# Halving projection and feed-forward pieces over two steps of a hand-ordered masked-attention kernel

## The chip, the cores and the metric

One core of a Trainium2 chip runs the whole program: 8 samples of a graph-attention layer with a feed-forward block. The metric is the device time of one execution in microseconds; lower is better.

## The reference, cut to what matters

For each of F = 8 samples (f), N = 2048 rows of C = 256 channels, H = 8 heads of D = 32 channels:

```python
qkv = jnp.einsum('fnc,ck->fnk', x, w_qkv)
...
scores = jnp.einsum('fnhd,fmhd->fhnm', q, k) / jnp.sqrt(jnp.asarray(D, x.dtype))
scores = jnp.where(mask, scores, jnp.asarray(-1000000000.0, x.dtype))
attn = jax.nn.softmax(scores, axis=-1)
t = jnp.einsum('fhnm,fmhd->fnhd', attn, v).reshape(F, N, C)
x = _layernorm(x + t, ln1_g, ln1_b)
h = jax.nn.relu(jnp.einsum('fnc,cd->fnd', x, w1) + b1)
f_out = jnp.einsum('fnd,dc->fnc', h, w2) + b2
x = _layernorm(x + f_out, ln2_g, ln2_b)
```

The mask is one 2048 x 2048 adjacency matrix, the same for all samples. A last layer norm of the input plus this result follows. All of it is float32.

## The kernel before, in words

**Items, steps and groups.** The attention is cut into 1024 items (f, qc, g, mb): sample f, a chunk qc of 512 query rows (4 of them), a set g of four heads (2), and a block mb of 128 key rows (16). The 16 items of one (f, qc, g) are called a group here; there are 64, numbered in order, and those with g = 0 are the even ones. The main loop (L455 to L478) takes one step per item. A step t writes, in this order, the instructions of

1. at most one job for the shared PSUM bank, taken from a list of unfinished work (`advance`, L386; not when mb is 0);
2. `scores` (L215) of item t + 2: four products on TensorE (L223) into two PSUM tiles, the mask added by VectorE in two instructions (L226) into a tile `p` in SBUF, and one exp on ScalarE (L228). It fills three rotating pairs of banks;
3. `values` (L232) of item t: four products (L240) that add up over the group's 16 steps in a bank of its own; at mb = 15 ScalarE copies the sum out (L244);
4. `add_up` (L253): the softmax denominators. The 16 `p` tiles of a group are not summed by TensorE one by one. GpSimd adds six of them onto the first (L260), and two chains of three are added by accumulating DMAs that GpSimd issues (L257), onto tiles 1 and 2. Four tiles remain: 14, 1, 2 and 0.

The `p` tiles come from a pool of 10 buffers. A buffer can be written again when its last reader is done: the values product, the addition on GpSimd or by DMA, or, for the four that remain, the ones-products (below).

**The shared bank.** Two banks change roles at each group: one holds the group's values, and the other is left for everything else. It has one buffer, so a job's first product waits until the result of the job before has been read out of it. The jobs:

- `turn` and `turn_rows` (L164, L155): transposes of an input chunk, L160, read out by ScalarE (L161);
- `queries` and `project`, both by `channels` (L177): 128 channels of 512 rows as two products, L180, read out by ScalarE (L182); and, in `project`, the values' projection as eight products of 128 columns, L205, read out by ScalarE (L208);
- `denominator` (L284): ones-products that add the four remaining tiles over the key rows, sixteen products L294 in two halves of eight, one per step, read out by ScalarE (L296) after the second; then a transpose L301 of that result, read by VectorE (L306 to L308);
- `outcome` (L313): two transposes L324, read by VectorE (L325), and a DMA issued by GpSimd that adds the input (L328);
- `tail` (L332): the layer norms and the feed-forward block: transposes L341 (ScalarE, L342), two hidden halves L352 (ScalarE, L353), two output halves L362 (VectorE, L364); between and after them `norm` (L263: VectorE L267 and L268, GpSimd L271 to L275, ScalarE L278), products and sums on GpSimd (L344, L346, L367, L369), an accumulating DMA (L371) and the store (L374, on SyncE's queue);
- in the first sample also the blocks of the mask (L136).

**What sets the order.** There is no scheduler: each engine executes in the order in which the program is written. The jobs are Python generators; `yield BANK` asks for the shared bank, `yield n` sleeps n steps, and other marks wait for input buffers or for a place among the tails. `fill` is sorted by due step. `advance` lets every generator run on as far as it can, and grants the bank to the first that asks, once per step. Denominators are due at once and go first, three steps into the next group when nothing is late. Where a projection is not written when its keys' scores come up, `advance` is called again within the step (L471). What is left after the last item is worked off at the end (L480).

Of the kernel before, what the change touches and what calls it, by code (L numbers as in the profile page):

```python
# [10 lines left out]
F32 = mybir.dt.float32  # L11
# [7 lines left out]
P = 128  # L19
H = 8  # L20
D = 32
CH = 512
# [3 lines left out]

SUM_MIN = 1e-25
SUM_MAX = 1e19
BANK, TURNED, ROOM, INPUTS = -1, -2, -3, -10

MASKED = -57344.0

# [21 lines left out]
def fast_path(ctx, tc, cst, x, adj, out, RS):  # L54
    nc = tc.nc
    F, N, C = x.shape
    NCK, TPC, MB = N // CH, CH // P, N // P
# [5 lines left out]
    kp = ctx.enter_context(tc.tile_pool(name="kp", bufs=2 * NCK + 2))  # L63
    qp = ctx.enter_context(tc.tile_pool(name="qp", bufs=2 * NCK + 2))
# [10 lines left out]
    ctx.enter_context(tc.manual_schedule())  # L75

    ident, identb, wqkv, w1s, w2s = cst["ident"], cst["identb"], cst["wqkv"], cst["w1s"], cst["w2s"]
    state = {"pair": 0, "side": None, "turn": 0, "turned": False, "tails": 0}

    def score_pair():  # L80
        i = state["pair"]
# [21 lines left out]
    def give(t):  # L103
        live[:] = [None if u is t else u for u in live]
# [42 lines left out]
    QT, KT, V, XT = {}, {}, {}, {}  # L147
    XD = [dp.tile([NCK, P, 2, CH], F32, name=f"xd{f}") for f in range(F)]

    def queries(f, c, xT):  # L150
        for g in range(2):
            yield BANK
            QT[f, c, g] = channels(qp, "qT", xT, g * P)

    def turn_rows(xc, xT):  # L155
        for a in range(2):
# [17 lines left out]
        yield from queries(f, c, xT)  # L174
        give(xT)

    def channels(pool, name, xT, k0):  # L177
        ps = bank()
        for a in range(2):
            nc.tensor.matmul(ps, wqkv[:, a, k0:k0 + P], xT[:, a, :], start=(a == 0), stop=(a == 1))  # L180
        t = pool.tile([P, CH], F32, name=name)
        nc.scalar.copy(t, ps)  # L182
        return t

    def reload(f, c):
        while (f, c) not in XT:
            yield 1
        yield INPUTS - 1
        xT = take([P, 2, CH], F32)
        nc.sync.dma_start(xT, XD[f][c])  # L190
        yield 3
        return xT

    def project(f, c, g, xT=None):
        if xT is None:
            xT = yield from reload(f, c)
            while len(KT) < (2 * f + g) * NCK + c:
                yield 1
        yield BANK
        KT[f, c, g] = channels(kp, "kT", xT, C + g * P)  # L200
        yield BANK
        ps = bank()
        for j in range(TPC):
            for a in range(2):
                nc.tensor.matmul(ps[:, j * P:(j + 1) * P], xT[:, a, j * P:(j + 1) * P],  # L205
                                 wqkv[:, a, 2 * C + g * P:2 * C + (g + 1) * P], start=(a == 0), stop=(a == 1))
        v = vp.tile([P, TPC, P], F32, name="v")
        nc.scalar.copy(v, ps.rearrange("p (j c) -> p j c", c=P))  # L208
        V[f, c, g] = v
        give(xT)  # L210
# [19 lines left out]
    LAST = MB - 1  # L230
# [53 lines left out]
    def denominator(f, qc, g):  # L284
        grp = (f, qc, g)
        terms = [PT.pop((f, qc, g, ALONE))] + [PT.pop((f, qc, g, chain[0])) for chain in MOVED + (POOLED,)]
        yield BANK
        ps = bank()
        for n, term in enumerate(terms):
            if n == 2:  # L290
                yield BANK
            for h in range(4):
                r = D * h
                nc.tensor.matmul(ps[r:r + D, :], cst["ones"], term[:, h, :], start=(n == 0), stop=(n == 3))  # L294
        dT = op.tile([P, CH], F32, name="dT")
        nc.scalar.copy(dT, ps)  # L296
        yield 1
        yield BANK
        ps = bank()
        for j in range(TPC):  # L300
            nc.tensor.transpose(ps[:, j * P:(j + 1) * P], dT[:, j::TPC], ident)  # L301
        if g == 0:
            RC[f, qc] = op.tile([P, TPC, H], F32, name="rc")
        rc = RC[f, qc]
        den = ps.rearrange("p (j c) -> p j c", c=P)[:, :, ::D]
        nc.vector.reciprocal(rc[:, :, 4 * g:4 * g + 4], den)  # L306
        nc.vector.tensor_tensor(RS[:, 0], RS[:, 0], den, ALU.add)
        nc.vector.tensor_tensor(RS[:, 1], RS[:, 1], den, ALU.min)  # L308
        if g == 1:
            begin = items.index((f, qc, g, LAST)) + SUM + 2  # L310
            start(begin, outcome(f, qc), begin)
# [20 lines left out]
    def tail(f, qc, y, xin):  # L332
        yield from norm(y)
        yield TURNED
        state["turned"] = True
        yT = work.tile([P, 2, CH], F32, name="turned")
        for a in range(2):
            yield BANK
            ps = bank()
            for j in range(TPC):  # L340
                nc.tensor.transpose(ps[:, j * P:(j + 1) * P], y[:, j, a * P:(a + 1) * P], ident)  # L341
            nc.scalar.activation(yT[:, a, :], ps, AF.Identity, bias=cst["be1c"][:, a:a + 1], scale=cst["g1c"][:, a:a + 1])  # L342
        yield 1
        nc.gpsimd.tensor_tensor(y, y, rows(cst["g1r"]), ALU.mult)  # L344
        yield 1
        nc.gpsimd.tensor_tensor(y, y, rows(cst["be1b2r"]), ALU.add)  # L346
        hT = work.tile([P, 2, CH], F32, name="hT")
        for d in range(2):
            yield BANK
            ps = bank()  # L350
            for a in range(2):
                nc.tensor.matmul(ps, w1s[:, a, d * P:(d + 1) * P], yT[:, a, :], start=(a == 0), stop=(a == 1))  # L352
            nc.scalar.activation(hT[:, d, :], ps, AF.Relu, bias=cst["b1s"][:, d:d + 1], scale=1.0)  # L353
        state["turned"] = False
        yield 1
        z = y
        for jj in range(0, TPC, 2):
            yield BANK
            ps = bank()
            for j in range(jj, jj + 2):  # L360
                for d in range(2):
                    nc.tensor.matmul(ps[:, (j - jj) * C:(j - jj + 1) * C], hT[:, d, j * P:(j + 1) * P], w2s[:, d, :],  # L362
                                     start=(d == 0), stop=(d == 1))
            nc.vector.tensor_tensor(z[:, jj:jj + 2, :], ps.rearrange("p (b c) -> p b c", c=C), z[:, jj:jj + 2, :], ALU.add)  # L364
        yield 1
        yield from norm(z)
        nc.gpsimd.tensor_tensor(z, z, rows(cst["g2r"]), ALU.mult)  # L367
        yield 1
        nc.gpsimd.tensor_tensor(z, z, rows(cst["be2r"]), ALU.add)  # L369
        yield 1  # L370
        nc.gpsimd.dma_start(z, xin, accum_op=ALU.add)  # L371
        yield 7
        yield from norm(z)
        nc.sync.dma_start(out[f, qc * CH:(qc + 1) * CH, :].rearrange("(p j) c -> p j c", p=P), z)  # L374
        state["tails"] -= 1


    fill = []
# [4 lines left out]

    def advance(t, banks):  # L386
        inputs = True
        for e in list(fill):
            while e[0] <= t:
                if e[2] == BANK:  # L390
                    if not banks:
                        break
                    banks -= 1
                elif e[2] < INPUTS:
                    inputs = inputs and not any(u is not None for u in live[:INPUTS - e[2]])
                    if not inputs:
                        break
                elif e[2] == TURNED and state["turned"] or e[2] == ROOM and state["tails"] == 2:
                    break
                e[2] = next(e[1], None)  # L400
                if e[2] is None:
                    fill.remove(e)
                    break
                if e[2] > 0:
                    e[0] = t + e[2]

    def mask_ahead(qc):
        for mc in range(NCK):
# [46 lines left out]
    for t, (f, qc, g, mb) in enumerate(items):  # L455
        if mb == 0 and t:
            state["side"] = 1 - state["side"]
        if f == 0 and g == 0 and mb == 0 and qc + 1 < NCK:
            start(t, mask_ahead(qc + 1), t + 28)
        if g == 1 and mb == 0 and (f or qc == NCK - 1) and (f + 1 < F or qc + 1 < NCK):  # L460
            load_mask(f + (qc + 1) // NCK, (qc + 1) % NCK)
        if f + 1 < F:
            for what, *which in NEXT.get((2 * qc + g, mb), []):
                due = t + MB // 2 if what is turn else items.index((f + 1, 0, which[1], which[0] * TPC)) - LEAD - 1
                start(t, what(f + 1, *which), due)
        if mb:
            advance(t, 1)
        if t + LEAD < len(items):
            nf, _, ng, nmb = items[t + LEAD]
            t0 = t  # L470
            while (nf, nmb // TPC, ng) not in V:  # L471
                advance(t0, 1)
                t0 += 1
            scores(items[t + LEAD])
        values(items[t])
        add_up(items[t])
        if mb == LAST:
            start(t + SUM, denominator(f, qc, g), t)  # L478
    t = len(items)
    while fill:  # L480
        t += 1
        advance(t, 1)


@with_exitstack
# [233 lines left out]
```

## Time and profile before

| | us |
|---|---|
| three timed runs | 3729.24, 3730.40, 3743.26 (median 3730.4) |
| the profiled execution | 3733.92 |
| its span, first to last instruction | 3732.1 |
| TensorE busy (PE) | 3241.8 |
| VectorE busy (DVE) | 2760.8 |
| GpSimd busy (POOL) | 2599.1 |
| ScalarE busy (ACT) | 2411.0 |
| granted TensorE clock | 0.977 of full |

Busy is the time in which an engine has an instruction running. PE rows are products, PEld rows weight loads. In the timeline each row has its start and its length in us, the engine, the line, what is written and read, and how many instructions were merged; in brackets stands how long the engine was idle before it and what ended that. A float32 product appears as two PE instructions, so that a job of two products 128x512 is x4, and a step's scores or values are x8.

### The profile page before, as it was taken

The numbers are of one execution on the slowest core, as the hardware profiler recorded it, in microseconds if no ns is written. First come the engines' busy times: TensorE is split into PE (matmuls) and PEld (weight loads), VectorE is DVE, ScalarE is ACT, GpSimd is POOL, SyncE is SP. The second block draws the span as 40 slices with busy tenths as digits, with TensorE's granted clock in tenths as the row PEclk, the third lists the DMA queues.
The fourth block names the chain that finished last, engine by engine and source line by source line (L and its number), as shares of the span: only waits on it lengthen the run. The fifth ranks groups of instructions, "written<-read, shape, count | busy, mean of one in ns | idle before, by whom it ended". The sixth has DMA issues, their size and how long they took to land. (4 is left out here: it accounts for less than half of the span.)

```text
span 3732.1 us, 53786 instructions
## 1 busy us (share of the span) xinstructions
PE 3241.8 (87%) x22020; PEld 1038.8 (28%) x22020; DVE 2760.8 (74%) x3203; ACT 2411.0 (65%) x1921; POOL 2599.1 (70%) x1363
## 2 busy tenths in 40 slices
PE   7877888899988899889998899889898889988884
PEld 4222223222322233222332223222232222322221
DVE  4777766877688766788677777777768877688883
ACT  3554555766667666766666776666666676677663
POOL 2555666777677775877667785777777777687775
PEclk9998999999999999999999999999999999999997
DMA  6766675776766775776766776676676676676664
GB/s 185 175 142 152 146 175 117 168 162 142 173 150 145 158 171 145 169 153 154 169 138 151 163 172 158 140 165 154 147 175 141 148 171 152 154 164 140 139 134 86
DMA packets 113774, 573.31 MB, mean 154 GB/s; under 512 B 10833, under 2 KB 27729, under 8 KB 60273
## 3 DMA queue, kind: packets, MB, share of 16 engines
q0 software_dynamic: 64848, 436.90, 58.1%
q1 hardware_dynamic: 47856, 131.61, 10.0%
q8 instruction: 174, 2.85, 0.3%
q10 hardware_dynamic: 816, 1.31, 0.1%
q14 instruction: 80, 0.65, 0.0%
HBM read 129.37 MB, written 37.75 MB: 45 GB/s over the span
## 5 line engine op out<-in xcount | busy, mean ns | idle before, releaser
L226 DVE TENSOR_TENSOR p<-s,mask 128x1024 f32<-128x1024 f32 x2048 | 2410.3, 1219 | 753.8 <-PE s L223 480.0
L228 ACT ACTIVATE p<-p 128x2048 f32<-128x2048 f32 x1024 | 1957.1, 1911 | 1232.9 <-DVE p L226 916.2
L260 POOL TENSOR_TENSOR p<-p 128x2048 f32<-128x2048 f32 x384 | 1835.9, 4810 | 653.6 <-ACT p L228 645.0
L223 PE MATMUL s<-qT,kT 32*128 32x512 f32 x8192 | 1193.2, 652 | 232.5 <-DVE p L226 231.0
L240 PE MATMUL x<-p,v 128*32 128x512 f32 x8192 | 1112.2, 616 | 0.0
L257 POOL DMA_DIRECT2D p<-p x384 | 382.7, 1018 | 351.2 <-ACT p L228 138.9
L223 PEld LDWEIGHTS s<-qT,kT 32*128 32x128 f32 x8192 | 325.3, 186 | 853.6 <-DVE p L226 695.6
L240 PEld LDWEIGHTS x<-p,v 128*32 128x32 f32 x8192 | 162.3, 108 | 795.2 <-issue 645.1
L180 PE MATMUL x<-in,wqkv 128*128 128x512 f32 x472 | 234.6, 620 | 23.1 <-ACT oT L244 10.2
L278 ACT ACTIVATE y<-y,nb,rs 128x256 f32<-128x256 f32 x384 | 224.9, 589 | 38.0 <-POOL nb L275 38.0
L294 PE MATMUL x<-p,ones 128*32 128x512 f32 x2048 | 246.3, 599 | 1.8 <-DVE y L364 0.9
L267 DVE BATCH_NORM_STATS2 st<-y 128x6 f32<-128x256 f32 x384 | 160.1, 417 | 27.1 <-DMA y<-in_x_dram 27.1
L362 PE MATMUL x<-w2s,hT 128*128 128x256 f32 x512 | 127.6, 392 | 45.7 <-ACT oT L244 42.3
L352 PE MATMUL x<-turned,w1s 128*128 128x512 f32 x256 | 128.8, 626 | 20.8 <-ACT hT L353 19.5
L180 PEld LDWEIGHTS x<-in,wqkv 128*128 128x128 f32 x472 | 80.3, 190 | 186.1 <-issue 69.8
L362 PEld LDWEIGHTS x<-w2s,hT 128*128 128x128 f32 x512 | 92.1, 190 | 112.0 <-ACT oT L244 68.6
L205 PE MATMUL x<-wqkv,in 128*128 128x128 f32 x896 | 114.9, 282 | 6.4 <-ACT kT L182 6.3
L205 PEld LDWEIGHTS x<-wqkv,in 128*128 128x128 f32 x896 | 104.2, 192 | 55.0 <-ACT kT L182 34.0
L364 DVE TENSOR_TENSOR y<-x,y 128x512 f32<-128x512 f32 x64 | 44.3, 692 | 94.9 <-PE x L362 94.7
L294 PEld LDWEIGHTS x<-p,ones 128*32 128x32 f32 x2048 | 64.0, 111 | 165.8 <-issue 129.7
L272 POOL TENSOR_TENSOR rs<-rs,mhalf 128x4 f32<-128x4 f32 x96 | 99.3, 1035 | 8.0
L341 PE MATMUL x<-ident,y 128*128 128x128 f32 x256 | 48.0, 299 | 54.5 <-ACT turned L342 38.8
(87 smaller groups left out, 1427.1 us busy)
## 6 DMA issues: line engine op xcount, KB each, us to landing
p<-p POOLq DMA_DIRECT2D x384, 1024.0 KB, 9.7
y<-in_x_dram POOLq DMA_DIRECT2D x64, 512.0 KB, 6.1
in<-xd SPq DMA_DIRECT2D x59, 512.0 KB, 8.0
mask<-md SPq DMA_DIRECT2D x28, 1024.0 KB, 6.6
out_dram<-y SPq DMA_DIRECT2D x32, 512.0 KB, 3.0
in<-in_x_dram SPq DMA_DIRECT2D x28, 512.0 KB, 6.9
xd<-in SPq DMA_DIRECT2D x28, 512.0 KB, 10.0
in<-in_adj_dram SPq DMA_DIRECT2D x24, 512.0 KB, 7.6
```

The source lines that it names most:

```text
L180: nc.tensor.matmul(ps, wqkv[:, a, k0:k0 + P], xT[:, a, :], start=(a == 0), stop=(a == 1))
L205: nc.tensor.matmul(ps[:, j * P:(j + 1) * P], xT[:, a, j * P:(j + 1) * P], wqkv[:, a, 2 * C + g * P:2 * C + (g + 1) * P], start=(a == 0), s ...
L223: nc.tensor.matmul(ps2[half][:, j, :], KT[f, mb // TPC, g][r:r + D, (mb % TPC) * P:(mb % TPC + 1) * P], QT[f, qc, g][r:r + D, :], start=Tr ...
L226: nc.vector.tensor_tensor(pt[:, 2 * half:2 * half + 2, :], ps, MK[f, qc][:, mb, None, :].to_broadcast([P, 2, CH]), ALU.add)
L228: nc.scalar.activation(pt, pt, AF.Exp, scale=1.0 / math.sqrt(D))
L240: nc.tensor.matmul(O[grp][r:r + D, :], V[f, mb // TPC, g][:, mb % TPC, r:r + D], PT[item][:, h, :], start=(mb == 0), stop=(mb == LAST))
L257: nc.gpsimd.dma_start(PT[f, qc, g, chain[0]], PT.pop(item), accum_op=ALU.add)
L260: nc.gpsimd.tensor_tensor(first, first, PT.pop(item), ALU.add)
L267: nc.vector.bn_stats(st, t[:, j, :])
L278: nc.scalar.activation(t[:, j, :], t[:, j, :], AF.Identity, bias=nb[:, j:j + 1], scale=rs[:, j:j + 1])
L294: nc.tensor.matmul(ps[r:r + D, :], cst["ones"], term[:, h, :], start=(n == 0), stop=(n == 3))
L362: nc.tensor.matmul(ps[:, (j - jj) * C:(j - jj + 1) * C], hT[:, d, j * P:(j + 1) * P], w2s[:, d, :], start=(d == 0), stop=(d == 1))
```

## The change

Three marks replace one: `BANK` asks for the bank as before; `MORE` and `HOLD` are given in the middle of a job whose bank is kept. The generator that keeps it is the `holder`. A job that reaches `MORE` goes on in the next step, before anything else, and in that step the bank is granted to nobody else. If, at the end of a step, another generator stands at `BANK` and is due to run, the holder at `MORE` is run on in the same step, so that its job stays whole. At `HOLD` (the ones-products, in the middle as before) it is not run on for another's sake. At the last step of a group, in the repeated calls for late projections and at the end (`finish`), any holder is run to its end. A generator that itself asks for the bank again after its job is not seen as waiting while it is the holder.

`MORE` stands in the middle of `channels` (after the first of two products), of the values' projection (after four of eight), of each hidden half (after the first of two) and of each output half (after two of four). The transposes are not divided. `channels` now stores its result itself.

```diff
-    def channels(pool, name, xT, k0):
+    def channels(store, pool, name, key, xT, k0):
+        yield BANK
         ps = bank()
         for a in range(2):
+            if a:
+                yield MORE
             nc.tensor.matmul(ps, wqkv[:, a, k0:k0 + P], xT[:, a, :], start=(a == 0), stop=(a == 1))
-        t = pool.tile([P, CH], F32, name=name)
-        nc.scalar.copy(t, ps)
-        return t
+        store[key] = pool.tile([P, CH], F32, name=name)
+        nc.scalar.copy(store[key], ps)
...
         for j in range(TPC):
+            if j == TPC // 2:
+                yield MORE
             for a in range(2):
...
             if n == 2:
-                yield BANK
+                yield HOLD
...
             for a in range(2):
+                if a:
+                    yield MORE
                 nc.tensor.matmul(ps, w1s[:, a, d * P:(d + 1) * P], yT[:, a, :], start=(a == 0), stop=(a == 1))
...
             for j in range(jj, jj + 2):
+                if j > jj:
+                    yield MORE
                 for d in range(2):
...
-    def advance(t, banks):
+    def resume(e, t):
+        e[2] = next(e[1], None)
+        state["holder"] = e if e[2] in (MORE, HOLD) else None if state["holder"] is e else state["holder"]
+        if e[2] is None:
+            fill.remove(e)
+        elif e[2] > 0:
+            e[0] = t + e[2]
+
+    def advance(t, free=True, finish=False):
         inputs = True
+        if state["holder"]:
+            free = False
+            resume(state["holder"], t)
         for e in list(fill):
-            while e[0] <= t:
+            while e[2] is not None and e[0] <= t and e is not state["holder"]:
                 if e[2] == BANK:
-                    if not banks:
+                    if not free:
                         break
-                    banks -= 1
+                    free = False
...
-                e[2] = next(e[1], None)
-                if e[2] is None:
-                    fill.remove(e)
-                    break
-                if e[2] > 0:
-                    e[0] = t + e[2]
+                resume(e, t)
+        late = any(e[2] == BANK and e[0] <= t for e in fill)
+        while state["holder"] and (finish or late and state["holder"][2] == MORE):
+            resume(state["holder"], t)
...
         if mb:
-            advance(t, 1)
+            advance(t, finish=mb == LAST)
...
             while (nf, nmb // TPC, ng) not in V:
-                advance(t0, 1)
+                advance(t0, finish=True)
...
-        advance(t, 1)
+        advance(t, finish=True)
```

More of the change, by code (lines that the diff above doesn't have):

```diff
@@ L28 @@
 SUM_MAX = 1e19
-BANK, TURNED, ROOM, INPUTS = -1, -2, -3, -10
+BANK, MORE, HOLD, TURNED, ROOM, INPUTS = -1, -2, -3, -4, -5, -10
 MASKED = -57344.0
@@ L77, in fast_path @@
     ident, identb, wqkv, w1s, w2s = cst["ident"], cst["identb"], cst["wqkv"], cst["w1s"], cst["w2s"]
-    state = {"pair": 0, "side": None, "turn": 0, "turned": False, "tails": 0}
+    state = {"pair": 0, "side": None, "turn": 0, "turned": False, "holder": None, "tails": 0}
     def score_pair():
@@ L151, in queries @@
         for g in range(2):
-            yield BANK
-            QT[f, c, g] = channels(qp, "qT", xT, g * P)
+            yield from channels(QT, qp, "qT", (f, c, g), xT, g * P)
     def turn_rows(xc, xT):
@@ L198, in project @@
                 yield 1
-        yield BANK
-        KT[f, c, g] = channels(kp, "kT", xT, C + g * P)
+        yield from channels(KT, kp, "kT", (f, c, g), xT, C + g * P)
         yield BANK
@@ L290, in denominator @@
             if n == 2:
-                yield BANK
+                yield HOLD
             for h in range(4):
```

## The prediction

> **What bounds the kernel now.** I read the page's first part and groups, then the timeline step by step, then the waits.
>
> ```profile
> PE 3241.8 (87%) x22020; PEld 1038.8 (28%) x22020; DVE 2760.8 (74%) x3203; ACT 2411.0 (65%) x1921; POOL 2599.1 (70%) x1363
> ...
> L226 DVE TENSOR_TENSOR p<-s,mask 128x1024 f32<-128x1024 f32 x2048 | 2410.3, 1219 | 753.8 <-PE s L223 480.0
> ```
>
> No engine is full: the bound changes from step to step. A step without a job lasts 2.55 us, and VectorE sets it: two mask additions of 1.22 us, TensorE 0.4 us idle.
>
> ```profile
> 1176.06 1.14 PE L223 MATMUL s<-qT,kT 32*128 32x512 f32 x8 [0.41 <-DVE p L226]
> ...
> 1177.34 2.36 DVE L226 TENSOR_TENSOR p<-s,mask 128x1024 f32<-128x1024 f32 x2 [0.20 <-PE s L223]
> ...
> 1178.62 1.14 PE L223 MATMUL s<-qT,kT 32*128 32x512 f32 x8 [0.42 <-DVE p L226]
> ```
>
> A step with a whole 2 us job is TensorE's, 3.98 us from job to job:
>
> ```profile
> 1655.74 1.98 PE L180 MATMUL x<-in,wqkv 128*128 128x512 f32 x4
> ...
> 1659.72 1.98 PE L180 MATMUL x<-in,wqkv 128*128 128x512 f32 x4
> ```
>
> By starts of rows (medians of the timeline), from the job to the scores it is 1.91 us for L180 and L352, 1.92 for L362, 1.98 for L205, 0.68 for L324; scores to values 1.07; values to the next job 1.00.
>
> The third bound is the bank. A job's result leaves it by a ScalarE copy, and that copy is written between two exps:
>
> ```profile
> 1646.84 1.14 PE L223 MATMUL s<-qT,kT 32*128 32x512 f32 x8
> ...
> 1648.90 0.66 PE L160 MATMUL x<-ident,in 128*128 128x128 f32 x4
> ...
> 1650.44 1.91 ACT L228 ACTIVATE p<-p 128x2048 f32<-128x2048 f32 x1 [1.15 <-DVE p L226]
> ...
> 1652.25 0.57 ACT L161 COPY in<-x 128x512 f32<-128x512 f32 x1
> ...
> 1652.87 0.66 PE L160 MATMUL x<-ident,in 128*128 128x128 f32 x4 [1.25 <-ACT in L161]
> ```
>
> The scores of 1646.84 are masked and exponentiated; only then is the job of 1648.90 copied out, and the next job may start at 1652.87, 1.25 us late. So a job starts no earlier than 6.03 us after the scores of two steps before. Over all triples of neighbouring jobs where this decides, the timeline has 6.03 to 6.82 us: 6.16 for L301 after the two L294 halves, 6.25 for L180 after L160, 6.63 for three L180, 6.73 behind an L352, whose own read-out is 0.67 us, 6.8 where a norm's L278 (0.59) stands between. I take 6.4 and keep 6.05 and 6.75.
>
> **What the Trainium skill says.** *TensorE: Matmul & The Clock Gate*, "Architectural detail", has ScalarE and VectorE as strict FIFO queues; the copy above, which starts when the exp ends, agrees. *PSUM — Partial Sum Buffer*, "The four PSUM rules", says that accumulation bits stay until the next first product of a group clears that bank and quadrant, so an open group may be left for a step; the L294 halves do that already, at 1.90 us each. *Perfetto Trace Analysis*, "Tensor Engine Instruction", says that matmul ends are estimated; hence I use starts.
>
> **The change, part by part.** The order of the changed program, counted step by step: 108 jobs are halved (70 L180, 20 L205, 15 L352, 3 L362); steps without a job fall from 333 to 230. Ones-products stay two halves in two steps: nothing.
>
> 1. *TensorE's side.* A half job from start to scores: L324 needs 0.68 for a quarter of the columns of a 1.91 job, so some 0.2 us is fixed and a half is 0.2 + 1.71/2 = 1.06. Two half steps: 2 x (1.06 + 1.07 + 1.00) = 6.26, against a whole and an empty step, 3.98 + 2.55 = 6.53. 108 x -0.27 = **-29 us**. VectorE, 2.4 of the 3.13 us, isn't in the way.
> 2. *The bank behind a second half.* In the order, 85 of the 108 are followed in the very next step by another job, after a read-out by ScalarE: a generator that wants the bank again doesn't count as waiting, so its halved jobs stand in a row. The next job's start is at least 1.06 + 6.4 = 7.46 us after the first half's; TensorE alone would take 6.26. Halving doesn't bring the copy forward: it sits behind the exp of the item whose scores ran with the first half. 85 x 1.20 = **+102** (72 to 132). Scores, values and VectorE's next masks queue behind that product.
> 3. *Such waits behind whole jobs.* Starts later than TensorE's pace add up to 13.9 us behind L180, 24.9 behind L352, 1.6 behind L205 now. Whole jobs of these kinds followed at once by a job fall from 81, 31, 19 to 11, 3, 12: 12 + 22 + 1 = **-35**.
> 4. *The second step of a group.* A job there waits for the copy L244 of the old values, on average 1.53 us past TensorE's pace (59.6 us in 39). 46 groups have one, not 39: **+11**.
> 5. *Late projections.* In the second sample, three steps get an L205 on top of other jobs because a half took its turn. Each waits within its step for the bank, up to 2 us beyond what it saves: **+4** (0 to 6).
> 6. *p buffers.* Jobs come later, so the ones-products start one to four steps later in 26 groups, and four old `p` tiles are held longer. The build's buffers show it: before, one group rewrites a buffer three items after its old tile, six times; after, 26 groups, 47 times (30 GpSimd additions, 17 DMAs). In that one group DMA reuse cost 1.43 and 5.04 us:
>
> ```profile
> 464.43 0.88 POOL L257 DMA_DIRECT2D p<-p  x1
> ```
>
> ```profile
> 475.57 2.36 DVE L226 TENSOR_TENSOR p<-s,mask 128x1024 f32<-128x1024 f32 x2 [5.04 <-DMA p<-p]
> ```
>
>    In the other even groups, item 3's addition ends 1.1 to 2.7 us before item 6 would write, so those hide. Item 4's DMA lands 1 to 4 us after item 7 starts, but the steps between grow about as much (two L362 ahead of the ones-products). I take 0.4 for each of 14 more by DMA: **+6** (0 to 45).
> 7. *Lag of GpSimd and its DMAs.* After the quickest even groups VectorE waits for such a buffer:
>
> ```profile
> 1183.67 2.36 DVE L226 TENSOR_TENSOR p<-s,mask 128x1024 f32<-128x1024 f32 x2 [0.88 <-DMA p<-p]
> ```
>
>    The first steps of odd groups run 37 us over 2.55 in samples 2 to 8, 33 net of shorter next steps. The even groups get longer (one of 48.9 us gains six 2 us jobs), so GpSimd catches up; L328, L367, L369 and L371 come up to three steps later, past the DMAs of tiles 7 and 10 and onto later additions. I count three quarters as regained: **-25** (-33 to 0).
> 8. *Queues and the end.* SyncE's queue holds as many instructions; stores L374, loads L190 and saves L171 shift by a few steps. Nothing there is late: inputs are asked for three steps ahead. If that cover went, a load's 8 us less three steps would show, under 1 us: zero. One more L362 is left after the last item: **+2**.
>
> Sum: -29 + 102 - 35 + 11 + 4 + 6 - 25 + 2 = **+36 us**. The profiled execution took 3733.9 (span 3732.1), so it would be 3770; on the median 3730.4 I predict **3766**, 1.0% slower.
>
> **Rivals.**
>
> - *Heavier: the `p` buffers decide.* If each of the 41 added close reuses costs what the one group showed, 6.5/6 = 1.1 us, item 6 is 45 instead of 6: **3805**. For it: accumulating DMAs there took 7 to 13 us, three quick steps are 7.6. Against: 27 of the 41 are additions of 4.8 us that end in time.
> - *Unchanged.* The bank's price at its low end, 6.05 (72), and all lag regained (-33): +36 - 30 - 8 = -2, **3728**. For it: plain copies without a norm beside them are nearer 6.05 to 6.25.
> - *Faster: the next job isn't held behind a second half.* The place is TensorE between a second half and the job after it, the price 85 x 1.20. A second half ends about 0.9 us earlier in its step than a whole job; were its copy to run ahead of the exp, item 2 would be nothing, the groups would not stretch (the 25 of item 7 stay lost): +36 - 102 + 25 = -41, **3689**. It decides when the wait is under 0.76 us a half for no change, under 0.55 for 0.5% faster, the other items kept. Against: exp and copy are in one queue, in the written order, and L301 behind the L294 halves, a split job already, waits just so.
> - *It doesn't do what it says:* excluded, the order shows the 108 halves.
>
> **How the numbers follow.** About 0.5% (19 us) is what a measurement can tell from no change. Forecast 0.58, heavier 0.12, both slower by more than that; unchanged 0.20; faster 0.10. So faster 0.1, same 0.2, slower 0.7. The range leaves out most of the faster case and the upper half of the heavier one: from 3724 (the unchanged case, 4 us under) to 3808. With price and lag at their bad ends together it would be 3820 and more; I leave that out. The forecast's own range is 3750 to 3795.
>
> **What would show it.** After: 230 empty steps of 2.55 us; half steps of about 3.1 us; after a second half, TensorE idle by about 1.2 us until ScalarE's copy, and the wait of L180 and L205 for ScalarE's qT and kT, 37 and 34 us of weight-load idle now, grown by some 80 in sum; less waiting of VectorE for DMAs at the first steps of odd groups, some at their items 7 to 10 in even ones; the 48.9 us groups at about 59. A half step well over 3.1 us, no idle TensorE after second halves, or jobs in other places would prove me wrong.

## The result and the profile after

The changed kernel takes 3796.8 us (median of four, 3793.8 to 3800.7), the kernel before, timed beside it, 3734.3 (3729.2 to 3743.3): a ratio of 1.0165, with a 95% interval of 1.0141 to 1.0189. That is 62.5 us slower. The profiled executions, from which all that follows is worked out, took 3796.24 and 3733.92 us, 62.3 apart.

The busy times of the page and the group of mask additions, for the changed kernel (lines are numbered by its own code: L182 was L180, L184 was L182, L207 was L205, L225 was L223, L228 was L226, L259 was L257, L262 was L260, L280 was L278, L326, L327 and L330 were L324, L325 and L328, L356 was L352, L373 and L375 were L367 and L369):

```profile
PE 3248.6 (86%) x22020; PEld 1034.2 (27%) x22020; DVE 2771.7 (73%) x3203; ACT 2411.1 (64%) x1921; POOL 2599.0 (68%) x1363
...
L228 DVE TENSOR_TENSOR p<-s,mask 128x1024 f32<-128x1024 f32 x2048 | 2409.5, 1218 | 835.6 <-PE s L225 482.7
```

No engine has more to do than before. VectorE's additions are as many and as long, but its idle time ahead of them grew from 753.8 to 835.6 us: the loss is waiting. The timeline shows the largest part of it (here both halves of an L182 and the job after them; brackets hold the idle time and what ended it):

```profile
1998.23 1.12 PE L182 MATMUL x<-in,wqkv 128*128 128x512 f32 x2
...
1999.29 1.14 PE L225 MATMUL s<-qT,kT 32*128 32x512 f32 x8
...
2001.35 1.13 PE L182 MATMUL x<-in,wqkv 128*128 128x512 f32 x2
...
2002.99 1.91 ACT L230 ACTIVATE p<-p 128x2048 f32<-128x2048 f32 x1 [0.69 <-ACT y L280]
...
2004.81 0.57 ACT L184 COPY kT<-x 128x512 f32<-128x512 f32 x1
2005.42 1.75 PEld L207 LDWEIGHTS x<-wqkv,in 128*128 128x128 f32 x15 [1.79 <-ACT kT L184]
```

The half step is as short as hoped: 3.12 us from 1998.23 to 2001.35. By the modelled ends the second half has left TensorE by 2002.5, but its copy L184 starts only at 2004.81, when the exp of 2002.99 has ended. The next job starts 4.07 us after the second half, 0.95 later than TensorE's pace.

Three sums over the whole trace are used below. *Bank waits*: start of a job, less the start of the values product of the step before, less 1.00 us (the sums are net: a job that starts a little sooner counts below zero). *Second-step waits*: the same at the second step of a group. *Buffer waits*: start of an item's first mask addition, less the later of VectorE's previous end and the scores' start plus 1.28 us (the distance from 1176.06 to 1177.34 in the prediction's first timeline); what is left is waiting for a `p` tile.

| kernel | time, us | ratio (95%) | bank waits | second step | buffer waits |
|---|---|---|---|---|---|
| before | 3734.3 | 1 | 157.5 | 59.6 | 43.8 |
| changed | 3796.8 | 1.0165 (1.0141 to 1.0189) | 202.8 | 68.3 | 64.2 |
| e2 exp late | 3544.2 | 0.9466 (0.9446 to 0.9486) | 2.4 | 2.1 | 80.9 |
| e4 before, exp late | 3558.6 | 0.9511 (0.9491 to 0.9531) | 7.7 | under 2 | 49.0 |
| e5 ones first, early store | 3815.8 | 1.0195 (1.0176 to 1.0215) | 214.8 | 70.3 | 42.3 |
| e7 before, ones late | 4062.4 | 1.0847 (1.0826 to 1.0868) | 258.6 | 60.4 | 303.8 |
| e12 addition 8 later | 3797.3 | 1.0149 (1.0132 to 1.0166) | 202.7 | 69.1 | 63.2 |

Beside the experiments the kernel before took 3738.5 to 3741.6 us, so times of different rows are compared by their ratios, or by profiled executions. The latter hold some noise of their own: the time ahead of the first values product, where all these programs have the same order but for the place of an exp, is 57.7 us in the profile of the kernel before, 60.2 in the changed one and 61.2 to 65.3 in the experiments. It is called the opening below, and differences of a few us between profiles show nothing. Of the changed kernel's bank waits 80.8 us lie behind second halves, where nothing lay before; those behind undivided L182, L356 and L207 fell from 40.4 to 10.9.

### The profile page after: what moved, and what is told of

The parts are those of the page before. It is cut to its first block, busy times and chain, and to the rows that moved or that the text cites. A ratio compares the mean times of both kernels' runs of the same rounds, so it can differ in the third digit from the quotient of the medians.

```text
span 3794.5 us, 53757 instructions
## 1 busy us (share of the span) xinstructions
PE 3248.6 (86%) x22020; PEld 1034.2 (27%) x22020; DVE 2771.7 (73%) x3203; ACT 2411.1 (64%) x1921; POOL 2599.0 (68%) x1363
## 5 line engine op out<-in xcount | busy, mean ns | idle before, releaser
L228 DVE TENSOR_TENSOR p<-s,mask 128x1024 f32<-128x1024 f32 x2048 | 2409.5, 1218 | 835.6 <-PE s L225 482.7
L262 POOL TENSOR_TENSOR p<-p 128x2048 f32<-128x2048 f32 x384 | 1804.0, 4698 | 643.9 <-ACT p L230 642.9
L225 PE MATMUL s<-qT,kT 32*128 32x512 f32 x8192 | 1191.3, 651 | 219.2 <-DVE p L228 217.0
L259 POOL DMA_DIRECT2D p<-p x384 | 358.9, 974 | 407.4 <-DMA p<-p 197.3
L225 PEld LDWEIGHTS s<-qT,kT 32*128 32x128 f32 x8192 | 325.2, 186 | 814.6 <-DVE p L228 672.4
L182 PE MATMUL x<-in,wqkv 128*128 128x512 f32 x472 | 253.6, 636 | 37.6 <-ACT qT L184 16.0
L280 ACT ACTIVATE y<-y,nb,rs 128x256 f32<-128x256 f32 x384 | 224.8, 589 | 41.8 <-POOL nb L277 41.8
L356 PE MATMUL x<-turned,w1s 128*128 128x512 f32 x256 | 132.4, 631 | 54.4 <-ACT oT L246 27.7
L207 PE MATMUL x<-wqkv,in 128*128 128x128 f32 x896 | 121.7, 286 | 35.4 <-ACT kT L184 19.1
L182 PEld LDWEIGHTS x<-in,wqkv 128*128 128x128 f32 x472 | 74.3, 188 | 224.6 <-issue 90.1
L207 PEld LDWEIGHTS x<-wqkv,in 128*128 128x128 f32 x896 | 107.2, 194 | 100.3 <-ACT kT L184 39.1
L296 PEld LDWEIGHTS x<-p,ones 128*32 128x32 f32 x2048 | 64.4, 110 | 173.9 <-issue 137.2
L343 PE MATMUL x<-ident,y 128*128 128x128 f32 x256 | 44.6, 293 | 63.7 <-ACT turned L344 43.9
L373 POOL TENSOR_TENSOR y<-y,g2r 128x1024 f32<-128x1024 f32 x32 | 83.6, 2611 | 12.8 <-ACT y L280 12.5
## 6 DMA issues: line engine op xcount, KB each, us to landing
xd<-in SPq DMA_DIRECT2D x28, 512.0 KB, 10.2
```

The lines of the kernel that those rows point to most:

```text
L225: nc.tensor.matmul(ps2[half][:, j, :], KT[f, mb // TPC, g][r:r + D, (mb % TPC) * P:(mb % TPC + 1) * P], QT[f, qc, g][r:r + D, :], start=Tr ...
L228: nc.vector.tensor_tensor(pt[:, 2 * half:2 * half + 2, :], ps, MK[f, qc][:, mb, None, :].to_broadcast([P, 2, CH]), ALU.add)
L259: nc.gpsimd.dma_start(PT[f, qc, g, chain[0]], PT.pop(item), accum_op=ALU.add)
L262: nc.gpsimd.tensor_tensor(first, first, PT.pop(item), ALU.add)
L280: nc.scalar.activation(t[:, j, :], t[:, j, :], AF.Identity, bias=nb[:, j:j + 1], scale=rs[:, j:j + 1])
```

## The experiments

### The bank behind the exp

**e2, the exp written later.** Nothing but the place of the exp in ScalarE's queue is changed; jobs, halves and buffers stay.

```diff
-        nc.scalar.activation(pt, pt, AF.Exp, scale=1.0 / math.sqrt(D))
+        state["exp"] = pt
+
+    def exp():
+        pt, state["exp"] = state["exp"], None
+        if pt is not None:
+            nc.scalar.activation(pt, pt, AF.Exp, scale=1.0 / math.sqrt(D))
...
             advance(t, finish=mb == LAST)
+        exp()
```

> The changed kernel with one edit: the exp of an item is written one step later, after the job of the next step and its read-out, ahead of the next scores; all else is in the same order. So a job's ScalarE copy no longer stands behind the exp of the item whose scores ran in the step before. Theory A, the bank is held behind the exp: the 81 us of waits behind second halves, and most of the 11 behind whole jobs and of the 45 and 48 behind the two kinds of transposes that ScalarE reads out, go; the time falls by 75 to 140 us, to 3655 to 3720. Theory B, the wait is not the exp's but the copy's own length and what VectorE does, or the later exp delays the values product as much: the time stays within 15 us of the changed kernel, or rises.

Measured: 3544.2 us, 5.3% below the kernel before; its profiled execution of 3543.3 is 253 us below that of the changed kernel. Theory A holds, and its estimate was far too low. At the same place of the program as above, the trace of this kernel (L235 is the exp):

```profile
1863.85 1.12 PE L182 MATMUL x<-in,wqkv 128*128 128x512 f32 x2
...
1865.01 0.59 ACT L184 COPY kT<-x 128x512 f32<-128x512 f32 x1 [0.71 <-PE x L182]
1865.95 1.91 ACT L235 ACTIVATE p<-p 128x2048 f32<-128x2048 f32 x1 [0.36 <-DVE p L228]
...
1866.97 1.86 PEld L207 LDWEIGHTS x<-wqkv,in 128*128 128x128 f32 x16 [0.84 <-issue]
```

Now ScalarE waits for the product and copies it at once; the exp follows at 1865.95, and the next job starts 3.12 us after the second half, not 4.07. Bank waits are gone (202.8 to 2.4; those behind second halves from 80.8 to nothing), and so are those of the second step (68.3 to 2.1), which I had not counted: the copy of the old values stood behind an exp as well. Together that is 266.6 us, of which buffer waits take 16.7 back.

**e4, the same edit on the kernel before** (nothing divided).

> The kernel before with the exp written one step later, after the next step's job and read-out; nothing is divided. If the bank behind the exp is what the division pays for, undivided jobs gain less from this edit than divided ones: they have 40 us of waits behind whole jobs and 98 us behind the two kinds of transposes, so the time falls by 50 to 120 us, to 3615 to 3685. Against the changed kernel with the same edit this shows what the division is worth once the bank wait is gone: by item 1 of the forecast 29 us, less 9 for the second step of a group and what the p buffers cost, so between 0 and 20 us in favour of the division. If the edit does nothing here, the transposes' waits are not the exp's.

Measured: 3558.6 us; between the profiled executions (3733.9 and 3554.5) 179 us. So much did the exp ahead of the copies cost without any halves. With the exp late, the division gains 11 us between the profiles and 0.45% by the ratios (0.9466 against 0.9511, the intervals just apart), within the 0 to 20 us expected: the sign of the change turns once the exp no longer stands ahead of the copies. Halving costs 62 us with the exp there and gains 11 without, so some 73 us of its cost hang on that one place.

**e10, only queries and keys divided** (the other three `yield MORE` removed), and **e9, only the values' projection divided** (the other three removed).

> The changed kernel with only the queries' and keys' projections divided: 71 halved jobs, 70 of them followed at once by another job. By the measured prices: 71 x -0.27 = -19 us; 70 x +0.92 = +64; whole jobs followed at once fall from 117 to 40 (L182 of the changed kernel) and from 61 to 38 (L356), some -17; second steps of a group with a job 47 instead of 39, +10; 3 more close reuses by DMA at 1.3, +4: +42 us, a ratio of 1.011. If bank waits were the smaller part of the loss and the pushed-back feed-forward and p buffers the larger, it is under +25, a ratio under 1.007, since close reuses are 24 instead of 47.

> The changed kernel with only the values' projection divided: 19 halved jobs, of which 6 are followed at once by another job, 12 close reuses of p buffers. Theory A, what costs is the bank behind a second half that a job follows: 19 x -0.27 = -5 us, 6 x +0.92 = +6, three more close reuses by addition and none by DMA: nothing; the time is that of the kernel before within 8 us, a ratio of 0.998 to 1.002. Theory B, each division costs by itself, wherever it stands (62.5 us over 108 halves, 0.58 each): +11 us, a ratio of 1.003.

e10: 1.0099 (1.0080 to 1.0119), 38 us between the medians and 42.5 between the profiled executions, near the sum of 42 by the measured prices and above the 25 of its rival. Bank waits behind second halves are 64.4 us in 70, the 0.92 each that were put in; that part of the sum is confirmed. The rest of the match is in part luck: 5.3 of the 42.5 us are the opening, and buffer waits fell by some 15 us where 4 more were expected. e9: 1.0051 (1.0032 to 1.0070), 20.3 us between the profiles, 5.1 of them the opening. That misses theory A's nothing and also B's 11. Its waits view names another wait, TensorE for a reloaded input (its L180 is the changed kernel's L182):

```profile
PE x L180 <- DMA in<-xd: 17.3, 6, 3.8
```

Six times the halves shift a load so that the product asks for it up to 3.8 us too early, 17.3 us in all (0.2 in the kernel before). Behind the six second halves that a job follows stand 5.6 us, as A has it. But the main loop, from the first values product to the last, grew by only 11 us, since buffer waits fell by some 12, and no run took the input's wait alone away; so e9 doesn't decide between A and B.

**e11, exp late with only the projections divided** (feed-forward whole).

> The changed kernel with the exp written after the next step's job, and the feed-forward pieces left whole: 91 halved projections, 243 empty steps, 25 close reuses of p (47 with all divided). With the exp late no bank wait is left, so each half that is not made costs the 0.27 us of item 1: 17 fewer, +5 us; the fewer close reuses and late projections give back some 10 to 20. So 3530 to 3542, if the p buffers count; 3544 to 3552 if not.

Measured: 3540.2 us, 0.9460 (0.9434 to 0.9486). That is at the upper end of the range for buffers that count, but from e2 it can't be told apart, so the time says nothing on the buffers. Both are the fastest versions found, 5.3 to 5.4% under the kernel before.

### The p buffers and the lag

**e1, ones-products first.** In 26 groups of the changed kernel they start late because a tail's due step ties with theirs and stands ahead in the list.

```diff
-            start(t + SUM, denominator(f, qc, g), t)
+            start(t + SUM, denominator(f, qc, g), t - 1)
```

> The changed kernel with one edit: the ones-products are due one step earlier in the list of work, so that they go ahead of the feed-forward jobs with which they tie. Counted in its order: 107 divided jobs and 230 empty steps as in the changed kernel, 89 of the 107 followed at once by a job (88 there), but ones-products begin at step 3 of the group in 60 of 62 groups (37 there), and close reuses of p buffers fall from 47 to 5. Theory A, the p buffers: the 30 us that bank waits and steps do not explain come from ones-products that start late and keep four old p tiles; then VectorE's waits for DMAs on p (56.7 us) and GpSimd's (197 us) go back to about 26 and 112, and the time falls by 20 to 35 us, to 3762 to 3777. Theory B, the forecast's own item 6: close reuses are nearly all hidden and cost 6 us, the rest is lag of GpSimd that was never regained; then the time is 3785 to 3797.

Measured: 3894.9 us, 1.0408 (1.0388 to 1.0427): 93 us slower than the changed kernel between the profiles, against both theories. The waits of VectorE show a place that was not in either:

```profile
DVE y L327 <- DMA out_dram<-y: 77.9, 21, 6.6
```

The feed-forward jobs now come later, so the tail's store leaves later, and the next outcome wants a `y` tile whose store has not landed; L327 stands in VectorE's queue, and bank waits behind the transposes L326 grow from nothing to 86 us. (The clock granted to TensorE was 0.968 in this run, against 0.977.)

**e3, both edits.**

> Both edits on the changed kernel: ones-products due one step earlier, and the exp written after the next step's job. If bank waits and p buffers are two separate costs, the two gains add up: the time is that of the changed kernel less the gain of each alone (within 10 us). If the p buffers' waits come only because bank waits push the ones-products, the second edit adds under 8 us to the gain of the first. By theory A of both, 3630 to 3695.

Measured: 3574.9 us, 0.9552 (0.9534 to 0.9571), 32 us slower than e2 alone between the profiles. The gains don't add, because the second is a loss.

**e5 and e8, the store three steps earlier**, to take that wait away: `yield 7` ahead of the last norm becomes `yield 4`, on e1 and on e3.

> The changed kernel with ones-products due one step earlier, as in the first experiment, and the pause ahead of a tail's last norm cut from 7 steps to 4, so that the tail's store is issued three steps earlier. In the first experiment VectorE waited 77.9 us (21 times) at the output of the next outcome for the store of an old y tile, and GpSimd and TensorE behind it. Theory A: that wait was the whole of the loss there, and below it the ones-products in time do save what late ones cost; close reuses of p stay at 5 instead of 47, so the 22 us of VectorE's waits at items 6 to 9 go to under 8, the wait for the store goes to under 5, and the time is 3770 to 3790. Theory B: feed-forward jobs pushed back cost as much by themselves (their additions on GpSimd fall on the start of odd groups); then it stays within 8 us of the changed kernel or is slower, 3790 to 3815.

> The changed kernel with the exp written after the next step's job, ones-products due one step earlier, and the pause ahead of the last norm cut from 7 steps to 4. The exp alone gave 3544. With the store in time the 26 us of waits behind outcome's transposes and VectorE's 19 us for the store of y are gone. If the p buffers are a cost of their own, 12 to 30 us are gained on the exp alone, 3514 to 3532; if not, the time stays within 8 us of 3544.

e5: 3815.8 us, 19 slower than the changed kernel between the profiles, 5 of them the opening, and with ratios whose intervals overlap; e8: 3560.7, 0.9510 (0.9485 to 0.9534), 15 slower than e2, 3 of them the opening. The wait for the store is down to 8.5 us in e5 and buffer waits fall by 22 us as expected (at items 6 to 9 from 24.4 to 7.9), and still the time doesn't fall. Against that gain stand 12 us more of bank waits and 7 at the end after the last item, where more is left. Some 15 us stay open; GpSimd now stands 95.8 us at L330 for the outcome's product (30.2 in the changed kernel) and 83.8 at L373 (12.5), but what of that reaches the path I could not separate. So late ones-products cost some 22 us at the buffers, and putting them first costs at least as much elsewhere.

**e7, late ones-products without halves.** On the kernel before, `start(t + SUM + 2, ...)`.

> The kernel before with one edit: ones-products may start two steps later (steps 5 and 6 of the group instead of 3 and 4), nothing is divided. Counted in the build: close reuses of p buffers 130 instead of 6, whole jobs followed by jobs hardly fewer (237 instead of 243). It prices the p buffers without divided jobs. By the trace of the changed kernel (some 21 us of added waits at items 6 to 9 for 41 added close reuses, 0.5 each) it is 62 us slower, about 3800; by the forecast's item 6 (6 us for 41) 18 us, 3755; by the heavier rival (1.1 each) 136 us, 3870.

Measured: 4062.4 us, 8.5% slower, above every estimate. Its waits of VectorE:

```profile
DVE p L226 <- DMA p<-p: 306.2, 82, 8.6
```

In the kernel before this line reads 25.8 us in 19 (19 waits, the middle number). Buffer waits rise by 260 us for 124 added close reuses, 2.1 each, most of it (some 220 us) at item 7, and bank waits by 101. (The clock granted to TensorE was 0.951 in this run, 0.977 in the two kernels compared.) A close reuse in an otherwise quick group costs twice what the heavier rival took. The changed kernel probably escaped because its late ones-products sit in groups that jobs have lengthened; no run tests that.

**e6, without scale and shift of the second norm.** L373 and L375 are left out, so the second norm's gain and shift aren't applied.

> The changed kernel without the scale and shift of the second layer norm (the multiplication L373 and the addition L375 on GpSimd, some 2.6 us each, are left out; the steps between are kept, so every other instruction has its place). In the changed kernel these two lie at steps 0 to 2 of the fourth and sixth group of a sample; before they lay at steps 14 and 15 of the third and fifth. VectorE's waits for p buffers there are 10.5 and 15.2 us over samples 2 to 8. Theory A, the lag wasn't regained but moved with these two: those 26 us fall to under 8 and the time by 20 to 35 us, to 3762 to 3777. Theory B, the lag comes from the chains of additions alone: the waits there stay over 15 us, and the time falls by under 12.

Measured: 3793.2 us, 1.0132 (1.0112 to 1.0151), not to be told from the changed kernel; waits at the start of the fourth and sixth groups 11.8 and 16.1 us, not less. My theory of the lag fell: these two additions aren't its cause.

**e12, GpSimd's addition of item 8 behind item 9's DMA.** In the changed kernel, the third group of the fifth sample ends so (GpSimd's part of the timeline, then VectorE's; L259 issues an accumulating DMA):

```profile
2107.09 2.11 POOL L259 DMA_DIRECT2D p<-p  x2
2109.16 4.62 POOL L262 TENSOR_TENSOR p<-p 128x2048 f32<-128x2048 f32 x1
2117.42 0.88 POOL L259 DMA_DIRECT2D p<-p  x1 [3.64 <-ACT y L280]
```

```profile
2122.65 2.36 DVE L228 TENSOR_TENSOR p<-s,mask 128x1024 f32<-128x1024 f32 x2 [2.27 <-DMA p<-p]
```

The x2 are the DMAs of items 9 and 10, 0.5 us apart; the single one is item 12's. The mask addition at 2122.65 is item 1 of the next group; in the build it takes the buffer of item 10, so it waits for that DMA to land.

```diff
-        if mb in POOLED[1:]:
-            first = PT[f, qc, g, POOLED[0]]
-            nc.gpsimd.tensor_tensor(first, first, PT.pop(item), ALU.add)
+        for pb in ([] if mb == 8 else [8, 9] if mb == 9 else [mb]):
+            if pb in POOLED[1:]:
+                first = PT[f, qc, g, POOLED[0]]
+                nc.gpsimd.tensor_tensor(first, first, PT.pop((f, qc, g, pb)), ALU.add)
```

> The changed kernel with one swap in GpSimd's queue: the addition of item 8 is written behind the DMA of item 9 instead of ahead of it; every other instruction keeps its place, and so do all buffers. In the changed kernel the third and fifth group of a sample became only 4.6 and 1.4 us longer (47.2 to 51.8, 50.3 to 51.7), while their DMA of item 9 is issued at 37.9 and 37.8 us of the group (32.3 and 33.9 before), behind the first norm, the input's DMA and the 4.8 us addition of item 8; the chain's last DMA, item 12's, waits for it and starts at 48.5, 3.3 us before the group ends. Theory A, VectorE's waits for p at the start of the next groups (10.5 and 15.2 us from sample 2 on) come from that place in the queue: item 9's DMA starts 3 to 4 us earlier, item 12's 2 to 4, the waits in these two groups fall from 25.7 to under 13, the time by 10 to 20 us: 3777 to 3787, a ratio of 1.011 to 1.014. Theory B, the transfers' own length decides, or the addition, now later, holds item 11's buffer instead: the waits stay over 20 or move on to items 10 and 11, and the time stays within 8 us of the changed kernel.

Measured: 3797.3 us, not to be told from the changed kernel. Item 9's DMA starts 1.2 us earlier in the third and 2.5 in the fifth group; the waits behind the third fall from 10.5 to 4.5 us, those behind the fifth stay (15.2, 15.4). So the queue's place is part of the cause in the third group. In the fifth it isn't: there, in samples 3 to 7, item 9's DMA lands 48.9 to 49.3 us into the group in both kernels, though it is issued 2 to 3 us earlier in this one. Something on the side of the DMAs decides there, theory B in the main; which transfers, no run shows. The DMAs of the third group above:

```profile
2110.61 1.22 POOL L259 DMA_DIRECT2D p<-p  x1
...
2115.70 1.58 POOL L259 DMA_DIRECT2D p<-p  x1
```

Here items 9 and 10 are 5.1 us apart, and item 10's lands 10.5 us after its issue, not 14.9. But it is also issued 3.1 us later in the group, so that it lands only 1.3 us earlier: a close issue made it wait longer and hardly land later.

## Why the prediction was right or wrong, step by step

Slower was right, and 3796.8 us lies in the range of 3724 to 3808, 1.8 us above the forecast's own range of 3750 to 3795. The sum on record was +36; the profiles differ by 62.3. By its steps:

| step | predicted | measured | how |
|---|---|---|---|
| 1 TensorE's side | -29 | -29 | 108 times 0.27: steps of second halves take 3.05 to 3.15 us, 3.13 predicted |
| 2 bank behind second halves | +102 | +81 | 80.8 us in 85, 0.95 each instead of 1.20 |
| 3 behind whole jobs | -35 | -30 | 40.4 to 10.9 |
| 4 second step of a group | +11 | +9 | 59.6 us in 39 to 68.3 in 46 |
| 5 late projections | +4 | +10 | three steps of 10.1, 8.1 and 5.9 us |
| 6 p buffers | +6 | +14 | buffer waits at items 5 to 15: 22 more at 6 to 9, 8 less later |
| 7 lag regained | -25 | +6 | buffer waits at items 0 to 4: 29.7 to 36.1 |
| 8 queues and end | +2 | +6 | after the last item 68.2 to 74.5 us |

These are +67; other bank waits, behind transposes above all, fell by 6: +61; the opening, 2.5 us longer in the changed kernel's profile, is not in them. Worked out the other way, the main loop less the three sums of waits became 21 us shorter, against -29 + 10. The agreement with 62.3 is closer than such sums deserve: in e4, with every job as before, the waits fell by 204 us and the main loop by 187. (For step 5: those three steps are 24.1 us; apart, the other jobs' steps would be 9.9, and each L207 step of 4.0 would take the place of an empty one of 2.55, 4.4 more for three.)

**Step 2** named the right mechanism: TensorE waits for a copy that stands behind an exp, and e2 shows it by moving that exp alone. Only its price was off. A next job starts 7.18 us after the first half of an L182, that is 6.12 after the scores; I took 6.4 and had 6.05 as the low end. Plain copies without a norm between are the rule (0.92 us of waiting a job behind L182, 0.90 behind L207), and the 1.16 behind L356 (6.36 from the scores) is the exception.

**Step 7** is the one that failed. I argued that even groups get longer, so that GpSimd catches up, and counted three quarters. That happened behind the first group of a sample (48.9 to 59.5 us; the waits behind it went from 10.2 to 0 over samples 2 to 8). But the third and fifth grew only from 47.2 to 51.8 and from 50.3 to 51.7 (from the last values product ahead of a group to its own last), and their DMA of item 9 was issued later by more than that: 5.6 us later in the group in the third, 3.8 in the fifth.

Item 10's DMA then lands 4.5 to 6.1 us after item 9's in these groups (samples 2 to 8 of the kernel before, the changed one and e12), whether it is issued 0.5 or 6.5 us behind it. So its landing moved with item 9's: in samples 3 to 7 from 1.3 to 1.9 us past the end of the third group to 1.9 to 2.7 past it, and at the fifth from 0.6 us ahead of the end, or 0.1 past it, to 1.9 to 2.3 past it. The first mask addition that takes its buffer waits for that, and the waits there went from 10.1 to 10.5 and from 3.5 to 15.2.

I had counted how much longer the groups get and not how much later the transfers start in them. *DMA: Bandwidth & Descriptors*, "Issuing engines are not separate DMA queues" in the Trainium skill, says that DMAs of all issuers run on the same 16 engines and interleave. That they share engines agrees with landings so far apart; but with its follower 0.5 us behind it, item 9's DMA in the third group took 9.7 to 10.4 us, no longer than before (9.6 to 10.8), so these two look more like taking turns than interleaving. No run separates the two.

**Step 6** was right on additions that end in time (0.7 us at item 6) and on most DMAs, but not on a few. Of 24.4 us at items 6 to 9, some 22 lie in five groups of the first two samples (4, 6, 7, 8 and 10, counted from 0), nearly 8 of them in group 7, an odd one, where step 6 speaks of even ones alone; in the later samples such waits are about 1 us in all. **Steps 1, 3 and 4** held within 5 us, step 3 not by its counts: whole jobs followed at once are 117, 61 and 42 in the trace before and 41, 25 and 36 after, where it has 81, 31, 19 and 11, 3, 12. In **step 8**, the cover of the loads held in the changed kernel (0.5 us of waiting for a reloaded input), though e9 shows that it is thin.

Steps 2 and 7 erred in opposite directions, -21 and +31, so the total is closer than its parts. The faster rival's point was right as a price: without the wait the change does gain (e2 against e4), but only 11 us, not 41. The heavier rival's time came close for another reason; its price of 1.1 a reuse is not what the changed kernel shows. (A slip in the first of these two: its break-even is 66 / 85 = 0.78 us a half, not 0.76.) One sign that I named was a poor one: the weight-load idle of L182 and L207 for qT and kT was to grow by 80 us and grew by 13 (37.1 and 34.0 to 44.6 and 39.1), since each such row has some 0.84 us of ordinary gap in it, and rows behind whole jobs left the list as others came. The starts in the timeline are the better view.

## What to carry to other kernels

Before a job is cut in two to smooth an engine, look at what frees its bank: here the read-out stood behind a long instruction of the same queue, and each cut that a job followed cost 0.95 us of waiting for 0.27 us of gain. The order within that queue was worth 179 to 253 us, the cutting 11 at best; a short copy that frees a shared resource goes ahead of a long instruction that still has slack. And where work is moved later, follow the buffers that it holds, and ask how much later its transfers start and land.

## What the runs showed of the hardware

Two accumulating DMAs of 1 MB between SBUF tiles, items 9 and 10 of the third and fifth groups of samples 2 to 8: the second landed 4.5 to 6.1 us after the first, whether issued 0.5 or 6.5 us behind it. Issued 0.5 us behind (samples 3 to 7), it took 14.1 to 14.9 us from issue to landing, against 9.2 to 10.2 in the kernel before with a lead of 5 us or more; the longer time was spent behind the first. An exp of 1.91 us written behind the next copy on ScalarE lengthened no step without a job (2.56 us, median, in e2), while waits for `p` tiles grew by 16.7 us in all.
